# A state-space scan and a convolution stage on one core: state copies in the scan's step, x projections with rising due times, and earlier due times for turns and exponentials

## The chip, the cores and the metric

The kernel runs on one core of a Trainium2 chip. Its engines are PE (TensorE: matrix products and transpositions), DVE (VectorE), ACT (ScalarE), POOL (GpSimd) and SP (SyncE, which here only issues DMAs). They run side by side, each through its own list of instructions in order, and wait for each other by semaphores. The metric is the time of one execution in microseconds (us); the median of three runs of the kernel before is 3147.45 us (3142.55 to 3149.4).

## The reference

Two layers, both added to their input. The first normalises each image over groups of channels, treats its 32 x 32 pixels as a sequence of L = 1024 steps and runs a selective state-space model over it. The second is an attention between two 3 x 3 convolutions. Cut to what matters here (B = 4 images, C = 512 channels, 1024 inner channels, 16 states):

```python
xs = silu(causal_conv4(xm) + conv_b)               # xm, z = halves of LN(x) @ W_in
proj = xs @ W_x                                    # 32 + 16 + 16 columns
dt = softplus(proj[..., :32] @ W_dt + b_dt)
Bm, Cm = proj[..., 32:48], proj[..., 48:]
def step(h, inp):                                  # over the 1024 steps
    dA = exp(dt_t[..., None] * A)
    h = dA * h + (dt_t * x_t)[..., None] * B_t[:, None, :]
    y = einsum('bds,bs->bd', h, C_t)
    return h, y
out = ((ys + xs * D) * silu(z)) @ W_out
```

The second layer computes two 1 x 1 and one 3 x 3 convolution, a softmax over all pairs of pixels, a weighted sum, and a last 3 x 3 convolution.

## The kernel before

**The first stage** works through the images one after the other. Channels lie on the 128 partitions; the 1024 inner channels are eight blocks, taken in four pairs `e`; the sequence is cut into two halves `h` of T = 512 steps. A *chunk* is one pair and one half (8 chunks an image, 32 in all, first half and second half in turn), and in it each of the 16 states `s` is a *unit*: 512 units. A unit (function `unit`) does this:

- ACT computes the decays exp(dt A), one [128, 512] instruction for each of the two blocks (line 746).
- The input term dt x B comes in one of two ways. For the ten states of `B_ON_ACT`, ACT scales rows of a transposed copy by B (line 758) and PE transposes the result back into a PSUM tile "u" (the *turn*, line 784). For the other six, POOL multiplies by B that a DMA has spread over the partitions (line 773), and the decays go into "u".
- DVE runs the recurrence with one scan instruction for each block (line 798). In the second half it starts from the state that the first half left in `carry_sb`.
- The product with C is made by POOL for both blocks at once (line 826), or by DVE for the three states of `C_ON_DVE` (line 814). PE adds the result into the PSUM tile "y" by transposing products (line 833).

In the first half the last column of each scan has to be kept in `carry_sb`. For the three states of `C_ON_DVE` each scan is followed, in the same step, by a copy of its own column (line 803, 128 x 1). For the other thirteen a step of its own copies the columns of both blocks in one instruction (line 820, 128 x 2), when both scans are done; the product with C overwrites the tile and so comes after it.

After the 16 units of a chunk `gate` turns y back and multiplies it by the gate. Other work of the same stage fills in: for the next image the norms (`norms`), the input projection with the four taps of the causal convolution on DVE (`conv1`, line 610), the gates' projection (`gates`), and the projection of xs to dt, B and C (`params`, line 652), which sums over the eight blocks for each half into one PSUM tile "pp"; for the image before, the output projection (`out_proj`); and 32 pieces of the transform of the second stage's convolution weights on POOL (`transform`, lines 1084 to 1119). `first_image` prepares the second stage's first image: it loads it, takes its statistics and normalises it.

**What sets the order.** No instruction of this stage is issued where it is written. Each is wrapped into a step with an engine, an estimated duration, the buffers that it reads and writes, and a due time in units (`prio`; a smaller number is more urgent). `Plan.issue` then walks through a model of the five engines: it takes, on the engine that is free first, the most urgent step that can start, books its duration, and writes the instruction down. Buffers that several steps share are rings; the rings "u" (four PSUM tiles, two units' worth), "h", "dbx", "sc", "cbc" and "bb" are handed out in the order of the program. "mm" (two PSUM tiles) serves the projections, the deltas and the gates. The due times of the fill work come from the dictionary `PRM`. The order on each engine is therefore fixed when the program is built; on the chip each engine follows it and waits where the estimate was off.

**The second stage** is written in order, from line 1180 on, and isn't touched by the diff, but for an engine order at its start that follows from when the first stage's tiles come free.

Of the kernel before, what the change touches and what calls it, by code (L numbers as in the profile page):

```python
# [20 lines left out]
NDC = DI // P  # L21
NS = 16
RK = 32
T = 512
# [3 lines left out]
GS = 16  # L28


PRM = dict(fi=4.61, m0=27.7, n0=50.77, nl=1.39, q0=50.1, qg=7.76, c0=53.17, cg=7.07, p0=120.48, e0=6.38, eg=3.72, g0=78.98, gg=9.04, o0=14.48, og=4.13, dl=9.01, t0=10, tg=21.42)


class Buf:
# [135 lines left out]
def mamba_then_pab_kernel(  # L170
# [25 lines left out]
    nc = tc.nc  # L196
# [67 lines left out]
    with ExitStack() as l0:  # L264
# [48 lines left out]
        carry_sb = wp.tile([P, 2, NS], F32, tag="carry", name="carry_sb")  # L313
# [24 lines left out]
        step = plan.step  # L338
        MM, TR = 0.88, 0.114
        ROWS, EXP, SCAN = 0.8, 0.61, 1.18  # L340
# [17 lines left out]

        proj = [buf(None, proj_sb[k * NP : (k + 1) * NP], "") for k in range(2)]
        bts = [buf(None, bt_sb[k], "") for k in range(2)]  # L360
        carry = [buf(None, None, "") for s in range(NS)]
        bcds = [buf(None, t, "") for t in bcd]
        szds = [[buf(None, None, "") for d in range(NDC)] for b in range(B)]
        gds = [[[buf(None, None, "") for h in range(NH)] for k in range(2)] for b in range(B)]
# [278 lines left out]
        def params(b, prio):  # L643

            p0 = b % 2 * NP
            pr = proj[b % 2]
            for h, hs in enumerate(halves):
                pp = buf("mm" if b else f"y{h}", [P, T], f"pp_{b}_{h}")
                for d in range(NDC):
                    step(  # L650
                        "PE", MM,
                        lambda d=d, hs=hs, pp=pp: nc.tensor.matmul(
                            pp()[p0 : p0 + NP, :], wx_sb[:, d, :], xs[b, d]()[:, hs],
                            start=(d == 0), stop=(d == NDC - 1),
                        ),
                        [xs[b, k] for k in range(NDC)] if b and d == 0 else [xs[b, d]], [pp],
                        prio if b else prio - 10 + d + 0.5,
                    )
                step(
                    "ACT", 0.48,  # L660
                    lambda hs=hs, pp=pp: nc.scalar.copy(pr()[:, hs], pp()[p0 : p0 + NP, :]),
                    [pp], [pr], prio,
                )
            step(
                "SP", 0.3, lambda: nc.sync.dma_start(bcd[b], pr()[RK:NP, :]),
                [pr], [bcds[b]], prio, kb=128,
            )
            pt = buf("mm", [P, NT, NP], f"pbt_{b}")

            def turn():  # L670
                for k in range(NT):
                    nc.tensor.transpose(
                        pt()[:, k, :], pr()[:, k * P : (k + 1) * P],
                        ident[p0 : p0 + NP, p0 : p0 + NP],
                    )

            step("PE", 8 * TR, turn, [pr], [pt], prio)
            bt = bts[b % 2]
            step(
                "DVE", 0.21, lambda: nc.vector.tensor_copy(bt(), pt()[:, :, RK : RK + NS]),  # L680
                [pt], [bt], prio,
            )
# [45 lines left out]
        def unit(b, e, h, s, y):  # L728


            dt, dtx, dtxt = dts[b, e, h]
            hs = halves[h]
            name = f"{b}_{e}_{h}_{s}"
            prio = (b * NDC + 2 * e + h) * NS + s
            bc = bcds[b]
            c_bc = buf("cbc", [P, 1, T], f"cbc_{name}")
            step(
                "SP", 0.32,
                lambda: nc.sync.dma_start(c_bc()[:, 0], bcd[b][NS + s][hs].partition_broadcast(P)),
                [bc], [c_bc], prio, kb=256,  # L740
            )
            us = [buf("u", [P, T], f"u_{name}_{j}") for j in range(2)]

            def decay(j, t):
                at = (2 * e + j) * NS + s
                nc.scalar.activation(t, dt()[:, j], AF.Exp, scale=a_sb[:, at : at + 1])  # L746

            on_act, on_dve = s in B_ON_ACT, s in C_ON_DVE
            if on_act:
                bt = bts[b % 2]  # L750
                sc = buf("sc", [P, NK, 2, P], f"sc_{name}")
                hc = buf("h", [P, 2, T], f"da_{name}")
                for r in range(2):

                    def rows(r=r):
                        for k in range(2 * r, 2 * r + 2):
                            at = h * NK + k
                            nc.scalar.activation(  # L758
                                sc()[:, k], dtxt()[:, k], AF.Copy, scale=bt()[:, at, s : s + 1]
                            )  # L760

                    step("ACT", ROWS, rows, [dtxt, bt], [sc], prio)
            else:
                b_bc = buf("bb", [P, 1, T], f"bbc_{name}")
                step(
                    "SP", 0.32,
                    lambda: nc.sync.dma_start(b_bc()[:, 0], bcd[b][s][hs].partition_broadcast(P)),
                    [bc], [b_bc], prio, kb=256,
                )
                hc = buf("dbx", [P, 2, T], f"dbx_{name}")  # L770
                step(
                    "POOL", 2.31,
                    lambda: nc.gpsimd.tensor_mul(hc(), dtx(), b_bc().to_broadcast([P, 2, T])),  # L773
                    [dtx, b_bc], [hc], prio,
                )

            parts = [buf(None, None, "") for j in range(2)]
            for j, u in enumerate(us):
                part = parts[j]
                if on_act:  # L780

                    def turn(j=j, u=u):
                        for k in range(NK):
                            nc.tensor.transpose(  # L784
                                u()[:, k * P : (k + 1) * P], sc()[:, k, j, :], ident
                            )

                    step(
                        "ACT", EXP, lambda j=j: decay(j, hc()[:, j]), [dt], [part], prio, "exp",
                        holds=[hc],  # L790
                    )
                    step("PE", 4 * TR, turn, [sc], [u], prio - 1)
                else:
                    step("ACT", EXP, lambda j=j, u=u: decay(j, u()), [dt], [u], prio - 1, "exp")

                def scan(j=j, u=u):
                    ht = u() if on_dve else hc()[:, j]
                    nc.vector.tensor_tensor_scan(  # L798
                        ht, *((hc()[:, j], u()) if on_act else (u(), hc()[:, j])),
                        carry_sb[:, j, s : s + 1] if h else 0.0, ALU.mult, ALU.add,  # L800
                    )
                    if h == 0 and on_dve:
                        nc.vector.tensor_copy(carry_sb[:, j, s : s + 1], ht[:, T - 1 : T])

                before, behind = ([carry[s]], []) if h else ([], [carry[s]] if on_dve else [])
                step(
                    "DVE", SCAN + (0.15 if behind else 0.0), scan,
                    [part if on_act else hc, u, *before],
                    [u if on_dve else part, *behind], prio - 1, holds=[hc],
                )  # L810
                if on_dve:
                    step(
                        "DVE", 0.6,
                        lambda j=j, u=u: nc.vector.tensor_mul(hc()[:, j], u(), c_bc()[:, 0]),
                        [u, c_bc], [part], prio, holds=[hc],
                    )
            if h == 0 and not on_dve:
                step(
                    "DVE", 0.15,
                    lambda: nc.vector.tensor_copy(carry_sb[:, :, s], hc()[:, :, T - 1]),  # L820
                    parts, [carry[s]], prio - 1, holds=[hc],
                )
            if not on_dve:
                step(
                    "POOL", 2.31,
                    lambda: nc.gpsimd.tensor_mul(hc(), hc(), c_bc().to_broadcast([P, 2, T])),  # L826
                    [c_bc], parts, prio, holds=[hc],
                )
            for j in range(2):

                def add(j=j):
                    for k in range(NK):
                        nc.tensor.matmul(  # L833
                            y[j]()[:, k, :], hc()[:, j, k * P : (k + 1) * P], ident,
                            start=(s == 0 and k == 0), stop=(s == NS - 1 and k == NK - 1),
                            is_transpose=True, skip_group_check=True,
                        )

                step("PE", 4 * TR, add, [parts[j]], [y[j]], prio, holds=[hc])

        def gate(b, e, h, y):

# [304 lines left out]
        for b in range(B):  # L1147
            at = b * NDC * NS
            for n in range(NDC):
                e, h = divmod(n, NH)  # L1150
# [401 lines left out]
```

## Time and profile before

| | |
|---|---|
| median of three runs | 3147.45 us |
| the profiled execution: time, span | 3152.2 us, 3150.4 us |
| first stage, from the first scan to the last | 166 to 2092 us |
| busy over the span: PE, DVE, ACT, POOL | 2801.1, 2324.9, 1896.9, 2185.6 us |
| granted TensorE clock, mean | 0.968 of full speed |
| DVE scans (L798), 128 x 512 | 1024, about 1.20 us in the first half, 1.26 in the second |
| POOL products of 128 x 1024 (L826, L773) | 608, 2.37 us each |
| DVE copies to `carry_sb`, 128 x 2 (L820) | 208, 83.8 us from "da" and 43.3 us from "dbx" |
| DVE copies to `carry_sb`, 128 x 1 (L803) | 96, 0.158 us each |

The span runs from the first to the last instruction, and the time lies around it. A line number such as L820 is the line of the kernel that issued an instruction. In an answer about waits, "A <- B: 47.4, 33, 7.5" means that A stood idle for B 47.4 us in total, 33 times, at most 7.5 us. In the tables of instructions the numbers after the tile names are the shortest, median and longest duration in ns, or the start and the duration in us in a timeline. [...]

### The profile page before, as it was taken

What the parts mean: (1) busy time and instruction counts of PE and PEld (TensorE: products, weight loads), DVE (VectorE), ACT (ScalarE), POOL (GpSimd) and SP (SyncE); (2) the same over time, 40 slices, a digit from 0 to 9 for tenths busy, and PEclk for the clock granted to TensorE, in tenths of its full rate; (3) what the DMA queues carried; (4) which work ended last, traced back from release to release, by engine and by line L of the source; (5) the groups of instructions that cost most, each with busy time, mean ns of one, the idle gap of its engine ahead of it and who ended that gap; (6) DMA issues with size and microseconds to landing.
All of it is one profiled execution on the core that took longest, in us unless ns stands there. A gap on an engine that the chain in (4) does not pass through costs nothing. (4 is left out here: it accounts for less than half of the span.)

```text
span 3150.4 us, 36613 instructions
## 1 busy us (share of the span) xinstructions
PE 2801.1 (89%) x11832; PEld 1654.8 (53%) x11832; DVE 2324.9 (74%) x2746; ACT 1896.9 (60%) x3322; POOL 2185.6 (69%) x1207
## 2 busy tenths in 40 slices
PE   4988878989888999888999877779999999999998
PEld 2455656666556656565655655544444444444443
DVE  3488899988999988999987987876275366447344
ACT  3499889998799999789998787752030030020000
POOL 8899898999969999978899998853052142224222
PEclk8999899999999999999999989989999999999999
DMA  6666455577645567745567654457268448628817
GB/s 190 192 186 195 144 152 162 156 226 241 212 118 169 163 204 250 231 114 155 165 192 227 204 172 123 121 139 263 93 225 312 183 147 317 257 74 312 321 61 253
DMA packets 401414, 600.03 MB, mean 190 GB/s; under 512 B 47176, under 2 KB 241992, under 8 KB 376648
## 3 DMA queue, kind: packets, MB, share of 16 engines
q1 hardware_dynamic: 392128, 582.13, 58.8%
q10 hardware_dynamic: 8936, 15.31, 1.3%
q8 instruction: 94, 1.54, 0.2%
q14 instruction: 96, 0.79, 0.1%
q0 software_dynamic: 160, 0.26, 0.0%
HBM read 500.60 MB, written 96.99 MB: 190 GB/s over the span
## 5 line engine op out<-in xcount | busy, mean ns | idle before, releaser
L826 POOL TENSOR_TENSOR da<-da,cbc 128x1024 f32<-128x1024 f32 x288 | 679.4, 2364 | 87.2 <-DVE carry_sb L820 47.4
L758 ACT ACTIVATE sc<-dtxt,bt_sb 128x256 f32<-128x256 f32 x1280 | 557.1, 496 | 49.3 <-PE u L784 48.8
L746 ACT ACTIVATE da<-dt,a_sb 128x512 f32<-128x512 f32 x640 | 439.4, 713 | 70.1 <-PE y L833 69.5
L773 POOL TENSOR_TENSOR dbx<-dtx,bbc 128x1024 f32<-128x1024 f32 x192 | 452.1, 2367 | 30.6 <-DMA bbc<-bcd 8.3
L784 PE MATMUL u<-ident,sc 128*128 128x128 f32 x2560 | 380.6, 282 | 52.4 <-DVE da L798 31.7
L833 PE MATMUL y<-ident,da 128*128 128x128 f32 x2560 | 357.3, 283 | 70.7 <-POOL da L826 68.2
L798 DVE TENSOR_TENSOR_SCAN da<-da,carry_sb,u 128x512 f32<-128x512 f32 x288 | 353.3, 1260 | 82.8 <-PE u L784 82.6
L833 PEld LDWEIGHTS y<-ident,da 128*128 128x128 f32 x2560 | 297.6, 145 | 183.4 <-POOL da L826 134.2
L784 PEld LDWEIGHTS u<-ident,sc 128*128 128x128 f32 x2560 | 302.2, 144 | 160.3 <-issue 41.7
L798 DVE TENSOR_TENSOR_SCAN da<-da,u 128x512 f32<-128x512 f32 x288 | 337.1, 1202 | 37.3 <-PE u L784 37.2
L1389 PE MATMUL m_b<-uw_b,v_b 128*128 128x512 f32 x768 | 339.1, 599 | 10.3 <-DMA uw_b<-u_b 9.4
L1389 PE MATMUL m_o<-uw_o,v_o 128*128 128x512 f32 x768 | 333.5, 595 | 4.3 <-DVE v_o L1311 4.1
L826 POOL TENSOR_TENSOR dbx<-dbx,cbc 128x1024 f32<-128x1024 f32 x128 | 302.8, 2365 | 32.1 <-DVE carry_sb L820 22.6
L381 PE MATMUL pxm<-xt,winc 128*128 128x344 f32 (+2 forms) x768 | 249.6, 469 | 30.5 <-DVE xs L610 13.9
L746 ACT ACTIVATE u<-dt,a_sb 128x512 f32<-128x512 f32 x384 | 252.9, 679 | 34.8 <-DVE da L798 18.9
L833 PE MATMUL y<-ident,dbx 128*128 128x128 f32 x1536 | 217.1, 281 | 43.7 <-POOL dbx L826 31.6
L381 PE MATMUL pz<-xt,winc 128*128 128x512 f32 x512 | 246.2, 599 | 10.5 <-ACT sz L631 3.1
L1389 PEld LDWEIGHTS m_b<-uw_b,v_b 128*128 128x128 f32 x768 | 144.7, 191 | 197.8 <-issue 185.7
L1389 PEld LDWEIGHTS m_o<-uw_o,v_o 128*128 128x128 f32 x768 | 145.5, 190 | 190.5 <-issue 181.2
L833 PEld LDWEIGHTS y<-ident,dbx 128*128 128x128 f32 x1536 | 178.4, 144 | 98.2 <-POOL dbx L826 48.6
L1437 PE MATMUL pat<-y_b,st 128*128 128x512 f32 x512 | 221.7, 593 | 0.1
L1397 ACT ACTIVATE e_b<-m_b 128x512 f32<-128x512 f32 x24 | 14.3, 596 | 320.6 <-PE m_b L1389 299.4
(231 smaller groups left out, 4536.2 us busy)
## 6 DMA issues: line engine op xcount, KB each, us to landing
cbc<-bcd SPq DMA_DIRECT2D x512, 256.0 KB, 3.7
uw_b<-u_b SPq DMA_DIRECT2D x96, 1024.0 KB, 4.9
uw_o<-u_o SPq DMA_DIRECT2D x96, 1024.0 KB, 4.9
bbc<-bcd SPq DMA_DIRECT2D x192, 256.0 KB, 4.1
u_b<-work SPq DMA_DIRECT2D x192, 128.0 KB, 2.3
u_o<-work SPq DMA_DIRECT2D x192, 128.0 KB, 3.1
winc<-in_w_in_dram SPq DMA_DIRECT2D x64, 256.0 KB, 3.8
szd<-sz SPq DMA_DIRECT2D x32, 512.0 KB, 3.6
```

The lines of the kernel that those rows point to most:

```text
L381: lambda k=k, lhs=lhs, rhs=rhs: nc.tensor.matmul(p()[:, at : at + cols], lhs(), rhs(), start=(k == 0), stop=(k == n - 1)),
L746: nc.scalar.activation(t, dt()[:, j], AF.Exp, scale=a_sb[:, at : at + 1])
L758: nc.scalar.activation(sc()[:, k], dtxt()[:, k], AF.Copy, scale=bt()[:, at, s : s + 1])
L773: lambda: nc.gpsimd.tensor_mul(hc(), dtx(), b_bc().to_broadcast([P, 2, T])),
L784: nc.tensor.transpose(u()[:, k * P : (k + 1) * P], sc()[:, k, j, :], ident)
L798: nc.vector.tensor_tensor_scan(ht, *((hc()[:, j], u()) if on_act else (u(), hc()[:, j])), carry_sb[:, j, s : s + 1] if h else 0.0, ALU.mul ...
L826: lambda: nc.gpsimd.tensor_mul(hc(), hc(), c_bc().to_broadcast([P, 2, T])),
L833: nc.tensor.matmul(y[j]()[:, k, :], hc()[:, j, k * P : (k + 1) * P], ident, start=(s == 0 and k == 0), stop=(s == NS - 1 and k == NK - 1), ...
L1389: nc.tensor.matmul(m[q], v[:, q, k, c, :], w[:, c, :], start=(c == 0), stop=(c == NCC - 1 and not extra),)
L1397: nc.scalar.activation(e, m[2], AF.Copy, scale=al / 2)
L1437: nc.tensor.matmul(pt, st[m][:, 2 * P * j + h : 2 * P * (j + 1) : 2], xb[m // 2][:, m % 2, :], start=(m == 0), stop=(m == NMC - 1),)
```

## The change

- **State copies.** The separate step of line 820 is gone. In the first half each scan's step now ends with a copy of its own last column (128 x 1) for every state; `carry` becomes one buffer for each state and block. The step's estimated duration is the scan's plus 0.14 for all states.
- **x projections.** In `params`, for images 1 to 3, the 16 matmuls of an image no longer share one due time: each is due 0.6 units after the one before (`pg`), from 112 units (`p0`, 120.48 before), and the copies to `proj` and what follows are due at the end of that.
- **Turns and exponentials.** The turns are due 2 units ahead of their unit (`kt`), the exponentials that go into "u" 1.91 units (`ke`); both were due 1 ahead. The additions to y are due 0.1 units later (`ka`).
- **Due times.** Eleven weight transforms instead of ten are due in the prologue (`t0`), `first_image` is due 21.48 units before the end instead of 4.61 (`fi`), and other entries of `PRM` move by small amounts (`fl` is used nowhere).

```diff
-PRM = dict(fi=4.61, m0=27.7, n0=50.77, nl=1.39, q0=50.1, qg=7.76, c0=53.17, cg=7.07, p0=120.48, e0=6.38, eg=3.72, g0=78.98, gg=9.04, o0=14.48, og=4.13, dl=9.01, t0=10, tg=21.42)
+PRM = dict(pg=0.6, kt=2, ke=1.91, ka=-0.1, fl=12.26, fi=21.48, m0=27.24, n0=50.77, nl=2.01, q0=44.34, qg=7.76, c0=53.52, cg=6.79, p0=112, e0=6.38, eg=2.48, g0=78.98, gg=9.04, o0=14.48, og=4.24, dl=9.01, t0=11, tg=21.45)
...
-        carry = [buf(None, None, "") for s in range(NS)]
+        carry = [[buf(None, None, "") for j in range(2)] for s in range(NS)]
...
-                        prio if b else prio - 10 + d + 0.5,
-                    )
+                        prio + PRM["pg"] * (d + NDC * h) if b else prio - 10 + d + 0.5,
+                    )
+                end = prio + (PRM["pg"] * NDC * (h + 1) if b else 0)
...
-                    [pp], [pr], prio,
-                )
+                    [pp], [pr], end,
+                )
+            prio = end
...
-                    step("PE", 4 * TR, turn, [sc], [u], prio - 1)
+                    step("PE", 4 * TR, turn, [sc], [u], prio - PRM["kt"])
                 else:
-                    step("ACT", EXP, lambda j=j, u=u: decay(j, u()), [dt], [u], prio - 1, "exp")
+                    step("ACT", EXP, lambda j=j, u=u: decay(j, u()), [dt], [u], prio - PRM["ke"], "exp")
...
-                    if h == 0 and on_dve:
+                    if h == 0:
                         nc.vector.tensor_copy(carry_sb[:, j, s : s + 1], ht[:, T - 1 : T])
 
-                before, behind = ([carry[s]], []) if h else ([], [carry[s]] if on_dve else [])
-                step(
-                    "DVE", SCAN + (0.15 if behind else 0.0), scan,
+                before, behind = ([carry[s][j]], []) if h else ([], [carry[s][j]])
+                step(
+                    "DVE", SCAN if h else SCAN + 0.14, scan,
...
-            if h == 0 and not on_dve:
-                step(
-                    "DVE", 0.15,
-                    lambda: nc.vector.tensor_copy(carry_sb[:, :, s], hc()[:, :, T - 1]),
-                    parts, [carry[s]], prio - 1, holds=[hc],
-                )
...
-                step("PE", 4 * TR, add, [parts[j]], [y[j]], prio, holds=[hc])
+                step("PE", 4 * TR, add, [parts[j]], [y[j]], prio - PRM["ka"], holds=[hc])
```

## The prediction

> **What bounds the kernel now.** I read the page first: in its forty slices the first 26 or so (the state-space stage, 0 to about 2092 us) have four engines between 80 and 100% busy at once, and the rest (convolution and attention) is PE alone. The change touches only the first part, so I cut that by batch with the table by stage (columns: us, then busy us of PE, PE weight loads, DVE, ACT, POOL, then clock and DMA).
>
> ```profile
> core 0: us, PE busy (x) PEld busy (x) DVE busy (x) ACT busy (x) POOL busy (x), PEclk, DMA share, GB/s
> 166.00:655.00 489.00, 423.57 (x2287) 291.86 (x2286) 436.24 (x518) 448.66 (x778) 444.09 (x243) 0.95 0.58 169
> 655.00:1147.00 492.00, 439.39 (x2358) 297.49 (x2357) 445.74 (x531) 440.06 (x769) 447.32 (x242) 0.98 0.61 185
> 1147.00:1637.00 490.00, 436.78 (x2359) 296.40 (x2357) 444.92 (x530) 439.00 (x768) 445.70 (x241) 0.98 0.62 186
> 1637.00:2092.00 455.00, 369.27 (x2079) 256.63 (x2078) 392.80 (x441) 349.01 (x648) 407.26 (x207) 0.95 0.60 172
> 2092.00:2123.00 31.00, 22.97 (x60) 11.43 (x58) 13.83 (x29) 10.59 (x18) 8.11 (x5) 0.74 0.25 82
> ```
>
> No engine owns a batch: ACT 92%, POOL 91%, DVE 91%, PE 89%. A batch takes 40 to 50 us more than its fullest engine, because steps come late for each other. So a saving on one engine counts only in part, and what matters is who is late. The waits between 166 and 2092 us (in total, times, longest):
>
> ```profile
> DVE da L798 <- PE u L784: 119.8, 42, 20.8
> ACT da L746 <- PE y L833: 69.5, 51, 4.9
> POOL da L826 <- DVE carry_sb L820: 47.4, 33, 7.5
> POOL dbx L826 <- DVE carry_sb L820: 22.6, 17, 5.3
> ACT u L746 <- DVE da L798: 18.9, 24, 1.6
> ```
>
> DVE waits for turns, and POOL for state copies. Looked at one by one, fourteen POOL waits of 1.5 to 7.5 us make 55 of the 70 us. Most lie where convolution taps, norms or products stand between the scans on DVE, and the copy in each takes 0.17 us or less: there DVE is late, not the copy. The view of the carry tile says what else copies cost:
>
> ```profile
> L820 DVE COPY carry_sb<-da x144: 157/242/2666, 168.6 to 2034.4; 128x2 f32<-128x2 f32 x144
> L803 DVE COPY carry_sb<-u x96: 157/158/163, 170.4 to 2021.1; 128x1 f32<-128x1 f32 x96
> L820 DVE COPY carry_sb<-dbx x64: 156/239/2366, 178.6 to 2028.2; 128x2 f32<-128x2 f32 x64
> ```
>
> A copy of two elements takes anything from 0.16 to 2.67 us, a copy of one never over 0.163. The timeline shows why: the copy of 942.01 ends when POOL's pair of multiplications ends (944.35), and the next scan waits behind it.
>
> ```profile
> 939.65 2.32 DVE L798 TENSOR_TENSOR_SCAN dbx<-u,dbx 128x512 f32<-128x512 f32 x2
> 942.01 2.37 DVE L820 COPY carry_sb<-dbx 128x2 f32<-128x2 f32 x1
> 944.29 2.32 DVE L798 TENSOR_TENSOR_SCAN da<-da,u 128x512 f32<-128x512 f32 x2
> ...
> 939.67 4.68 POOL L826 TENSOR_TENSOR da<-da,cbc 128x1024 f32<-128x1024 f32 x2
> ...
> 895.29 1.22 DVE L798 TENSOR_TENSOR_SCAN u<-u,dbx 128x512 f32<-128x512 f32 x1
> 896.54 0.16 DVE L803 COPY carry_sb<-u 128x1 f32<-128x1 f32 x1
> 896.62 1.22 DVE L798 TENSOR_TENSOR_SCAN u<-u,dbx 128x512 f32<-128x512 f32 x1
> ```
>
> **The Trainium skill.** "SBUF — State Buffer", Who interferes with whom: a DVE instruction in a two-port mode and a GpSimd instruction lock each other out for a whole instruction, copies among them. "VectorE: DVE Perf Modes", What auto-detection actually checks: a single-source copy within SBUF takes the two-port mode when its outermost dimension longer than one is even. A two-element copy qualifies; that a one-element copy doesn't is my reading, and the rows above agree with both (2666 against 163 ns). The same page, The DRAIN you can't avoid: DVE drains after every instruction, and reading what the previous one wrote takes a wait. The trace agrees: two scans without carry follow each other at 1.13 us, a scan and its own copy take 1.33.
>
> **The change part by part**, against the profiled execution (span 3150.4, time 3152.2 us).
>
> *State copies.* In first-half chunks, 13 of 16 states lose the joint copy of two elements (16 chunks x 13 = 208 instructions) and get one single-element copy after each scan (416); DVE issues 208 more. Busy time: 127.0 us of joint copies (83.8 + 43.3) against 416 x 0.158 = 65.7. Occupancy counts, since a copy also holds up the next scan: where a pair of scans and its joint copy run without a gap, start to next start is 2.81 us in the mean (median 2.51, longest 4.92), against 2 x 1.33 = 2.66. Saved: 208 x 0.15 = 31 us of DVE. The usual unit becomes 0.15 us longer; the blocked ones win up to 2.2. DVE and POOL are equally full, so I put half on the path: -16. Ends: 0 (POOL or ACT sets the pace) and -31.
>
> *Turns and exponentials ahead.* Turns (due one unit ahead) become due two ahead, exponentials of the GpSimd-scaled states 1.91 ahead; nothing is added. The DVE waits for turns are 119.8 us, less the opening one of 20.8: 99. They can't all go: the four "u" buffers hold just two units, and between 1100 and 1147 us PE itself is busy 46.56 of 47 us. I take a third, 33 us of DVE, half on the path: -16. Ends 0 and -50. Behind a turn that waits for a buffer stand the y additions, for which ACT's next exponentials wait (69.5 us); behind an early exponential the scaled rows that feed the next turns. That is the slower rival.
>
> *x projections.* The same 32 PE passes a batch (about 16 us at 0.5) run, by the changed program's order, over units 105-121 instead of 111-121 in batch 0, and 235.5-249 instead of 243-249 in batch 1; the copy to "proj", the store to "bcd", its transposition and the next deltas still follow at their end. Two or three us of PE leave the crowded last chunk: -5 for three batches. Against it, a projection tile holds one of the two "mm" buffers some 7 units longer; with about five handovers more at one copy (0.575) and a gap (0.2) each it is 4 us a batch, +12 at worst. Ends +12, -15.
>
> *Prologue.* One more weight transform stands before the first dtx on POOL (11 against 10): 12.3 us into a gap of 10.4 us (141.5 to 151.9). POOL has 10 us less to do later, its first dtx is 2 late: -5. Ends 0, -10. Its DMAs leave SP in the same prologue; their number in all stays.
>
> *First image.* Its 8 loads on SP, 4 memsets on POOL, 12 statistics, 4 normalisations come before the last chunk's scans on DVE instead of after them. Off the join: the table loads and root that held PE for 4.6 us at 2107, and statistics ahead of the last gate; -7. But 5.6 + 3.0 us of DVE work enter a last chunk in which DVE is already 100% busy, with 9 us of idle DVE in the chunk before to absorb part: +5. In the next stage's order the input transform of the first convolution comes behind two more POOL operations of about 2.5 us and interleaves with the maxima: +2. Sum 0; ends -9, +8.
>
> *Norms, convolutions and gates* move by a few units (batch 1's norms 6 units earlier with wider steps; its gates end 8 units earlier). The same instructions; they fill gaps between scans, so 0. If that cover went, a norm's 16 DVE operations of 0.74 us, 12 us, would be exposed once.
>
> Sum: -16 - 16 - 5 - 5 + 0 = -42: a span of 3108 and a time of 3110. The profiled execution lies 4.75 over the median of the runs (3147.45), so the median is **3106 us**, 1.3% less.
>
> **Rivals.** (1) *Larger gain*: late DVE work is what leaves POOL idle (70 us), and the blocked copies made it late. If POOL ran 95% of each batch, as it already does in good stretches (48.13 of 50 us from 1150), the four batches take 1744 / 0.95 = 1836 instead of 1926: -90, 3058. Against: ACT would have to run at 96% in batch 0. (2) *No gain that shows*: the DVE time freed turns into DVE idling, because ACT (448.66 of 489) and POOL need their time anyway; 3147. Against: the copies lie in front of POOL's largest waits. (3) *Slower*: exponentials of the GpSimd-scaled states get in line early and wait at ACT's head for a "u" buffer, which DVE must free. Today 26.7 us of such waits in 38 (18.9 + 7.8 for the other kind), 0.7 us each, of 384 exponentials. Of 96 in a batch, if 60% wait, it is 40 us a batch, what ACT has spare; beyond that each adds to the time. At 80%, 54 us, some 14 us too much in three batches of ACT-heavy work: 3147 + 42 less half the other gains, 3168. Against: the planner's order lets ACT take other ready steps first. (4) That the copies don't lose their blocking is excluded by the 96 rows of one-element copies.
>
> **How the numbers follow.** Mine 0.60 (its own range 3080 to 3138: ends of the parts, not all at once), larger gain 0.22, no gain 0.07, slower 0.11. So faster by over 0.2% (below 3141) is 0.82, within it 0.07, slower 0.11; 0.2% is about what a measurement of this kernel can tell from no change. The range 3055 to 3142 takes the larger gain and leaves out no gain and slower.
>
> **What would show it.** Right: all copies of carry at 128x1 and 0.157 to 0.163 us, about 80 us of DVE in all with the 96 old ones; DVE's wait for turns under 80 us; POOL's wait behind carry copies about halved; batches of about 480 us; after the last scan, scores starting within 25 us instead of 31.6. Wrong: ACT waits for "u" above 60 us, PE waits for "mm", batches still near 490 with DVE idling more.

## The result, and the profile after

The changed kernel takes 3105.64 us in the median of four runs (3100.51 to 3108.2); the kernel before, run beside it, 3148.43 (3142.55 to 3156.02). The ratio is 0.9861, with a 95% interval of 0.9836 to 0.9886. That is 0.4 us from the forecast. The experiments show that the sum came out right, but not its parts.

The table by stage of the changed kernel, cut at its own batches (columns as before: us, then busy us of PE, PE weight loads, DVE, ACT, POOL, then clock and DMA):

```profile
core 0: us, PE busy (x) PEld busy (x) DVE busy (x) ACT busy (x) POOL busy (x), PEclk, DMA share, GB/s
163.00:649.00 486.00, 429.39 (x2300) 296.02 (x2299) 423.71 (x571) 454.92 (x787) 442.48 (x242) 0.95 0.59 170
649.00:1129.00 480.00, 436.71 (x2354) 301.88 (x2353) 430.48 (x582) 436.22 (x765) 449.79 (x244) 0.97 0.64 191
1129.00:1604.00 475.00, 438.97 (x2359) 304.68 (x2358) 430.55 (x582) 436.63 (x766) 444.52 (x241) 0.96 0.64 192
1604.00:2058.00 454.00, 369.87 (x2071) 254.13 (x2070) 394.30 (x513) 350.46 (x649) 395.01 (x199) 0.95 0.58 167
```

The span is 44.1 us shorter (3150.4 to 3106.3). By the starts of the scans, 3.0 of it lie before the first scan (166.2 to 163.2), 30.8 in the four batches (489.2, 491.9, 490.0, 454.2 became 485.8, 480.2, 474.9, 453.6, so nearly all in the second and third), and the rest after the last scan (1058.9 to 1048.7). DVE works 12 to 15 us less in each of the first three batches; there ACT and POOL have about the work that they had.

The waits of the changed kernel between 163 and 2058 us (in total, times, longest), those that answer to the rows shown of before:

```profile
DVE da L800 <- PE u L786: 102.6, 45, 20.6
ACT da L748 <- PE y L829: 55.1, 44, 5.1
POOL da L822 <- DVE carry_sb L805: 35.7, 24, 5.3
POOL dbx L822 <- DVE carry_sb L805: 22.9, 12, 6.0
ACT u L748 <- DVE da L800: 8.9, 13, 1.6
```

Four of the five are smaller, one (22.6 before) is as large as it was, none is gone: DVE's wait for turns fell from 119.8 to 102.6 us, POOL's for state copies, both rows together, from 70.0 to 58.6. The view of the carry tile:

```profile
L805 DVE COPY carry_sb<-da x288: 152/154/158, 164.4 to 1994.9; 128x1 f32<-128x1 f32 x144
L805 DVE COPY carry_sb<-dbx x128: 152/154/156, 173.6 to 1988.4; 128x1 f32<-128x1 f32 x128
L805 DVE COPY carry_sb<-u x96: 157/158/160, 167.1 to 1980.7; 128x1 f32<-128x1 f32 x96
```

There are 512 copies instead of 304, and none takes over 0.160 us, although 412 of them start and end inside one POOL instruction. This also settles what the rows of before left open. There all 96 one-element copies read the PSUM tile "u", so they differed from the two-element copies in the memory that they read as well as in the number of elements. Here 416 copies read "da" and "dbx" in SBUF, 328 of them inside a POOL instruction, and they take 0.152 to 0.158 us. The timeline shows two of them: both copies lie inside POOL's pair of products, 885.02 to 889.69, and neither is held up.

```profile
885.01 1.21 DVE L800 TENSOR_TENSOR_SCAN da<-da,u 128x512 f32<-128x512 f32 x1
886.26 0.15 DVE L805 COPY carry_sb<-da 128x1 f32<-128x1 f32 x1
886.33 1.21 DVE L800 TENSOR_TENSOR_SCAN da<-da,u 128x512 f32<-128x512 f32 x1
887.57 0.15 DVE L805 COPY carry_sb<-da 128x1 f32<-128x1 f32 x1
...
885.02 4.67 POOL L775 TENSOR_TENSOR dbx<-dtx,bbc 128x1024 f32<-128x1024 f32 x2
```

### The profile page after: what moved, and what is told of

Read it like the earlier page. It is cut to its first block, busy times and chain, and to the rows that moved or that the text cites. A ratio compares the mean times of both kernels' runs of the same rounds, so it can differ in the third digit from the quotient of the medians.

```text
span 3106.3 us, 36781 instructions
## 1 busy us (share of the span) xinstructions
PE 2799.1 (90%) x11832; PEld 1666.2 (54%) x11832; DVE 2259.1 (73%) x2954; ACT 1893.6 (61%) x3321; POOL 2175.4 (70%) x1207
## 4 chain that ended last, share of the span: by engine, by line
PE 42%; DVE 16%; POOL 6%; issue 4%; ACT 4%; DMA 4%; SPq 0%; POOLq 0%; DVEq 0%; ACTq 0%
PE m_o L1385 9%; PE m_b L1385 8%; PE pat L1433 7%; DVE da L800 6%; PE y L829 4%; PE po L381 3%; DVE dbx L800 3%; PE pz L381 2%; PE u L786 2%; DMA uw_b<-u_b 2%; DVE u L800 2%; POOL da L822 2%; PE psc L1265 2%; ACT sc L760 1%; POOL dbx L822 1%
## 5 line engine op out<-in xcount | busy, mean ns | idle before, releaser
L800 DVE TENSOR_TENSOR_SCAN da<-da,u 128x512 f32<-128x512 f32 x288 | 349.2, 1212 | 48.1 <-PE u L786 44.8
L381 PE MATMUL pxm<-xt,winc 128*128 128x341 f32 (+2 forms) x768 | 244.2, 462 | 18.0 <-ACT xt L557 9.0
L829 PE MATMUL y<-ident,dbx 128*128 128x128 f32 x1536 | 223.6, 286 | 25.8 <-POOL dbx L822 17.9
```

Source lines behind the costliest of these rows:

```text
L381: lambda k=k, lhs=lhs, rhs=rhs: nc.tensor.matmul(p()[:, at : at + cols], lhs(), rhs(), start=(k == 0), stop=(k == n - 1)),
L800: nc.vector.tensor_tensor_scan(ht, *((hc()[:, j], u()) if on_act else (u(), hc()[:, j])), carry_sb[:, j, s : s + 1] if h else 0.0, ALU.mul ...
L829: nc.tensor.matmul(y[j]()[:, k, :], hc()[:, j, k * P : (k + 1) * P], ident, start=(s == 0 and k == 0), stop=(s == NS - 1 and k == NK - 1), ...
```

## The experiments

The diff does two things that come together in the profile: it alters the copies, and, through its due times and the planned length of the steps, it alters the order on every engine. So the first group of runs holds the order fixed and alters the copy alone; the second alters due times; the third alters the order and nothing else. No experiment leaves any of the computation out. All ratios are to the kernel before, measured beside the run.

### The copy alone, with the order of every engine held

**1. The order before, the joint copy replaced by two copies of one column at the same place.**

```diff
-                    lambda: nc.vector.tensor_copy(carry_sb[:, :, s], hc()[:, :, T - 1]),
+                    lambda: [
+                        nc.vector.tensor_copy(carry_sb[:, j, s : s + 1], hc()[:, j, T - 1 : T])
+                        for j in range(2)
+                    ],
```

> The kernel before, in its own order on every engine; only the joint two-element copy is replaced by two one-element copies at the same place. Theory A (a two-element copy waits for POOL's instruction, and the scans behind it pay): no copy over 0.17 us, DVE gains about 0.25 us a unit (2.81 against two scans at 1.13 and two short copies, about 2.56), 52 us in all, half of it on the path: 15 to 30 us faster than before. Theory B (the order that the planner makes is what pays, the copies were covered): within 6 us of before.

Measured: 3105.21 us (3100.97 to 3108.67), ratio 0.987 (0.9857 to 0.9884), against 3145.34. The copy alone, with no due time touched, brings 40 us: as much as the whole change, and more than the 15 to 30 expected. DVE is busy 2247.3 us instead of 2324.9. The carry tile of this kernel:

```profile
L821 DVE COPY carry_sb<-da x288: 120/144/156, 164.6 to 1986.2; 128x1 f32<-128x1 f32 x144
L821 DVE COPY carry_sb<-dbx x128: 125/143/156, 173.8 to 1980.2; 128x1 f32<-128x1 f32 x128
```

And DVE's waits for turns in it, which are as large as before:

```profile
DVE da L798 <- PE u L784: 126.2, 45, 21.1
```

**2. The changed order, with a joint copy in the step of the second block's scan.**

```diff
-                    if h == 0:
+                    if h == 0 and on_dve:
                         nc.vector.tensor_copy(carry_sb[:, j, s : s + 1], ht[:, T - 1 : T])
+                    if h == 0 and not on_dve and j == 1:
+                        nc.vector.tensor_copy(carry_sb[:, :, s], hc()[:, :, T - 1])
```

> The changed kernel in its own order on every engine, but the thirteen states that had a joint two-element copy have it again, in the step of the second block's scan. A: copies of 0.16 to 2.6 us come back, and the kernel is 10 to 25 us slower than the changed one (about 3120 to 3130). B: within 6 us of the changed kernel (about 3105).

Measured: 3156.72 us (3151.01 to 3162.89), ratio 1.0034 (1.0022 to 1.0047). With all else of the change in place the joint copy makes it slower than before: 51 us behind the changed kernel, where 10 to 25 were expected. DVE is busy 2345.3 us. The carry tile, and the timeline round the longest copy:

```profile
L807 DVE COPY carry_sb<-da x144: 168/224/3341, 169.9 to 2049.8; 128x2 f32<-128x2 f32 x144
L807 DVE COPY carry_sb<-dbx x64: 168/245/2380, 179.7 to 2043.7; 128x2 f32<-128x2 f32 x64
```

```profile
781.92 2.31 DVE L800 TENSOR_TENSOR_SCAN da<-da,u 128x512 f32<-128x512 f32 x2
784.26 3.34 DVE L807 COPY carry_sb<-da 128x2 f32<-128x2 f32 x1
787.52 1.22 DVE L800 TENSOR_TENSOR_SCAN u<-u,dbx 128x512 f32<-128x512 f32 x1
...
782.86 4.72 POOL L824 TENSOR_TENSOR da<-da,cbc 128x1024 f32<-128x1024 f32 x2
```

The copy starts in the first of two products that follow each other on POOL, and ends with the second (787.60 and 787.58); the next scan stands behind it for over 3 us.

**3 and 4. One copy of both columns that isn't a copy instruction**: a maximum over a dimension of length 1, which moves the same two elements, first in the changed order, then in the order before.

```diff
-                        nc.vector.tensor_copy(carry_sb[:, :, s], hc()[:, :, T - 1])
+                        nc.vector.reduce_max(carry_sb[:, :, s], hc()[:, :, T - 1 : T], axis=AX.X)
```

> As the run before, but the two last columns are taken by one maximum over a dimension of length one, a reduction instead of a copy. If only the copy's two-port mode is blocked by POOL (A), this instruction stays at about 0.16 us and comes once in a unit: pair and copy at about 2.46 us instead of 2.66, 42 us less of DVE, half on the path, 10 to 25 us faster than the changed kernel (about 3085 to 3095). B: the same as the changed kernel. If reductions are blocked too: as with the joint copy.

> The kernel before in its own order, with the joint copy made by a reduction over a dimension of length one (one instruction, not held up by POOL). Theory A' (about half of each us of DVE saved is gained): DVE as in the run with two single copies (a pair with its copies 2.44 us in both), so about 3105. Against the changed kernel with the same reduction (3092) it shows what the new due times alone are worth once the copies are no matter: 13 us if A' holds.

Measured: in the changed order 3092.34 us (3089.53 to 3096.94), ratio 0.9831 (0.9818 to 0.9845), faster than both kernels; in the order before 3104.29 (3102.16 to 3106.45), ratio 0.9871 (0.9857 to 0.9884). The carry tile of the former:

```profile
L807 DVE TENSOR_REDUCE carry_sb<-da x144: 156/157/160, 164.9 to 1979.2; 128x2 f32<-128x2 f32 x144
L807 DVE TENSOR_REDUCE carry_sb<-dbx x64: 156/157/159, 173.6 to 1971.6; 128x2 f32<-128x2 f32 x64
```

Same two elements, same place, same neighbours on POOL: 0.160 us at most instead of 3.341. So with two elements it is the kind of instruction that decides: the copy is held up, the reduction isn't. With copies it is the number of elements: two are held up, one isn't (run 1). The Trainium skill ("SBUF — State Buffer", Who interferes with whom) says that on this chip a reduction has no two-port mode and never contends with GpSimd, while a copy can; these two runs agree with both halves.

Together (us; a cell is the median of its kernel):

| form of the copy | order before | changed order |
|---|---|---|
| joint, 128 x 2 | 3147.45 | 3156.72 |
| two of 128 x 1 (changed order: each behind its own scan) | 3105.21 | 3105.64 |
| joint, as a reduction | 3104.29 | 3092.34 |

Down a column the order is the same. Across the first and the third row the copy is the same; in the middle row its place differs too, so that row doesn't show the order alone. Down, the copy is worth 40 us in the order before (3145.34 beside it) and 51 in the changed one. Across, the other parts of the change together cost some 11 us with the joint copy and bring 12 with the reduction.

Two reservations. The changed kernel was measured in another session than runs 1 to 3, and the kernel before read 3.1 us higher in it; by the ratios the 51 us are 54, and the 13 us from the changed kernel to run 3 are 9. And the granted clock goes along with the times: 0.960 to 0.961 in run 2, 0.967 to 0.970 in the changed kernel, 0.972 to 0.973 in run 3. For the same work in the four batches PE was busy 12 us longer in run 2 than in the changed kernel, and 19 us less in run 3. Whether that is a part of the cause or a consequence isn't shown.

### Parts of the due times

**5. The copies alone, as the change makes them, with all due times of before**: the changed code with `kt=1, ke=1, ka=0, pg=0` and the other entries of `PRM` as they were.

> The own copy in each scan's step with its planned 0.14 us, and all due times as before: the planner makes a new order. The prediction: -16 us against before, ends 0 and -31. B: the gain of the copies alone is nothing, within 6 us of before.

Measured: 3144.44 us (3134.67 to 3149.0), ratio 0.9995 (0.9988 to 1.0002): no gain. The copies are as short as in the changed kernel (none over 0.16 us). Against run 1 two things differ: the place of the first block's copy, and the order, which the planner worked out anew. So when the planner works the order out anew, the copies alone bring nothing, and the due times on top of them bring 39 us (3144.44 to 3105.64); with the order held it is the other way round. What a part of the change is worth depends on the order in which it stands. The joint copy wasn't run in this order, so what the form of the copy is worth there isn't known.

**6. The changed kernel without the look-ahead.**

```diff
-PRM = dict(pg=0.6, kt=2, ke=1.91, ...
+PRM = dict(pg=0.6, kt=1, ke=1, ...
```

> The changed kernel with turns and exponentials due one unit ahead again (kt and ke at 1), all else as changed. The prediction: the look-ahead is worth 16 us (0 to 50), so about 3121, and the waits of DVE for turns go up from 82 us by about a third. Rival (the order as such is luck): anywhere within 15 us on either side, with no more waits for turns.

Measured: 3138.9 us (3132.9 to 3151.26), ratio 0.9981 (0.997 to 0.9992). Taking the look-ahead away costs 33 us. POOL now waits 98.8 us behind state copies instead of 58.6, and DVE for turns 106.9 instead of 102.6: the waits by which this part was priced hardly move.

```profile
DVE da L800 <- PE u L786: 106.9, 53, 20.5
POOL da L822 <- DVE carry_sb L805: 84.2, 33, 10.6
POOL dbx L822 <- DVE carry_sb L805: 14.6, 9, 3.5
```

**7. The look-ahead alone, on the kernel before**: `kt=2, ke=1.91`, all else as before, joint copies in their own step.

> The kernel before with one part of the change alone: turns and exponentials two units ahead; joint copy, projections, first image and all other due times as before. Theory 1 (the form of the copy and the look-ahead each pay by themselves): the look-ahead is worth about what its removal from the changed kernel cost, 33 us, so 3105 to 3125 us, with the DVE's waits for turned tiles well below the 120 us of before. Theory 2 (the look-ahead pays only once the copies no longer hold the DVE up, because until then the scans are late for another reason): 3138 to 3152 us, with the joint copies still at a mean of 200 ns and more.

Measured: 3177.89 us (3176.71 to 3184.65), ratio 1.0104 (1.0088 to 1.0121), against 3147.62. By itself it makes the kernel 30 us slower, which neither theory had. DVE is as busy as before (2327.6 and 2324.9 us), and so are its state copies (143.7 and 142.2), so these aren't held up more; all four batches are longer (494.4, 500.1, 499.6, 462.6). The granted clock was lower, 0.961 to 0.963 against 0.968 to 0.972, and PE was busy 18 us longer in the four batches; what is cause here and what consequence isn't shown.

**8. The x projections as before**: the changed kernel with `pg=0, p0=120.48`.

> The changed kernel with all sixteen x projections of an image due at once at 120.48 units again. The prediction: spreading is worth 5 us (from 15 gained to 12 lost), so about 3110. Rival: the two PSUM tiles held longer cost more than the spreading gives, and this is faster than the changed kernel by up to 12 us.

Measured: 3120.52 us (3115.14 to 3125.58), ratio 0.9924 (0.9911 to 0.9938): 15 us slower than the changed kernel.

**9. The first image as before**: the changed kernel with `fi=4.61`.

> The changed kernel with the first image due 4.61 units before the end again; the order differs only in the last quarter of the stage. The prediction: nothing in sum (7 us gained at the join, 5 lost in the last chunks, 2 in the first convolution), so within 6 us of 3105. By the trace of the changed kernel the time from the last scan to the end is 10 us shorter than before (1048.6 against 1058.9 us) and the last two chunks are 6 us longer (115.5 against 109.0): this run should give both back, 0 to 5 us slower.

Measured: 3105.04 us (3101.12 to 3106.94), ratio 0.9872 (0.9858 to 0.9885): no difference. In the profile both halves of the trade can be seen. The last two chunks take 109.7 us instead of 115.4, and what follows the last scan 1055.5 instead of 1048.7.

**10. All the changed due times, with the joint copy in its own step**, planned anew.

> All the changed due times, look-ahead, spreading and first image, but the joint 128x2 copy in its own step as before, and the order planned anew. Theory 1 (the copies' form is most of the gain, and the due times are worth some 12 us, as the two orders differ with the one-instruction copy that is not held up): 3130 to 3140 us. Theory 2 (the due times only serve the order with own copies, as the joint copy put into the changed order gave 3157): 3145 to 3160 us. Theory 3 (the due times are most of the gain): 3105 to 3120 us.

Measured: 3162.25 us (3156.66 to 3165.28), ratio 1.0047 (1.0032 to 1.0062). All due times without the copies make it 15 us slower, as run 2 did by 11 in another order.

### The order and nothing else

**11. The same work, planned with another number**: the own copy is planned at 0.15 us instead of 0.14.

```diff
-                    "DVE", SCAN if h else SCAN + 0.14, scan,
+                    "DVE", SCAN if h else SCAN + 0.15, scan,
```

> The changed kernel with one number of the planner altered: the own copy is planned at 0.15 instead of 0.14 us. No work differs, only the order on each engine. Theory 1 (an order that comes out differently by chance moves the time by less than 0.2%): 3099 to 3112 us. Theory 2 (the due times fit one order, and any other order loses part of the gain): 3115 to 3140 us; then differences of 10 to 30 us between kernels with different orders can't be put down to a part of the change.

Measured: 3127.82 us (3123.75 to 3129.71), ratio 0.9938 (0.9924 to 0.9952): 22 us slower than the changed kernel, with the same work (only ACT loads a function table 174 times instead of 176) and the same granted clock (0.966 to 0.970). 428 of 2442 positions on DVE, copies apart, hold another instruction. The table by stage shows the work spread over longer batches.

```profile
653.00:1139.00 486.00, 438.43 (x2362) 299.25 (x2359) 430.63 (x583) 433.61 (x765) 437.34 (x232) 0.97 0.62 186
1139.00:1623.00 484.00, 434.77 (x2352) 298.53 (x2352) 430.79 (x582) 434.69 (x763) 443.70 (x240) 0.97 0.63 188
```

In the second batch DVE has 430.63 us of work, 430.48 in the changed kernel, ACT 433.61 against 436.22, and POOL 12 us less, of which 7 were done in the first batch; yet it takes 485.4 us instead of 480.2, the third 484.8 instead of 474.9. This is the price of another order, which nobody chose. The variants of the changed kernel whose orders the planner worked out anew in runs 5, 6, 8 and 10 are slower than it by 15 to 57 us, and run 7 is 30 slower than the kernel before. Each holds the effect of its part and of such another order together, and one order for each can't tell the two apart. None of these orders came out faster than the one it is compared with, so the scatter isn't even to both sides: the changed kernel has a good order among those that were tried, and why it is good isn't shown.

**12. The reduction, with the planner told of it**: the first block's scan planned without a copy, the second's with 0.14 us, the order worked out anew.

```diff
-                    "DVE", SCAN if h else SCAN + 0.14, scan,
+                    "DVE", SCAN + (0.14 if not h and (on_dve or j) else 0.0), scan,
```

> The changed kernel with one copy of both columns as a maximum over a dimension of length 1, behind the second block's scan, and the planner told so: the first block's scan planned without a copy, the second's with 0.14 us; the order is planned anew. Theory 1 (a plan that counts what the DVE really does gives an order at least as good): 3075 to 3092 us. Theory 2 (the order matters by chance as much as by plan): 3092 to 3125 us; the copies themselves 156 to 160 ns in either case.

Measured: 3117.11 us (3115.67 to 3122.97), ratio 0.9911 (0.9895 to 0.9927). A plan that is closer to what DVE does came out 25 us slower than run 3, whose order was planned for other copies. That is the second theory, and the second sight of what another order costs.

## Why the prediction was right, and where it was not

**The number was right, and that it was so close is luck: the copies brought far more than they were given, the rest less, by about as much.** The sum was -16 for the copies and -26 for all else: -16 for the look-ahead, -5 for the projections, -5 for the prologue and 0 for the rest. Measured with the order held, the copies are worth -40 to -51, outside their ends of 0 and -31. One path takes the two parts in turn: from the kernel before to run 2 everything changes but the form of the copy, +11; from run 2 to the changed kernel that form alone, -51. By the table the rest is +11 to -12, and -26 was predicted. On the other path, where the planner makes a new order at each step, the copies are worth -1 (run 5) and the due times -39. Neither path gives the shares of the sum.

**State copies: mechanism right, half on the path about right, size of the DVE term wrong.** That two-element copies are held up by POOL and one-element copies aren't is shown by runs 1 and 2, and runs 3 and 4 show that it takes the copy instruction. One step of the argument was not sound, though it came out true: the 96 one-element copies of before couldn't exclude rival (4), since they all read PSUM. "Half on the path" held up: 40.1 us for 77.6 of DVE (0.52) in run 1, 41.0 for 87.9 (0.47) in run 4, 51.1 for 86.2 (0.59) from run 2 to the changed kernel, 13.3 for 28.7 (0.46) from there to run 3. By the ratios the last two are 0.63 and 0.33; and from run 1 to run 4 DVE has 10 us less and the time is the same within 1 us. So half is a rough mean, not a rule.

What failed is "208 x 0.15 = 31 us of DVE". It set the pitch of the joint copy in the order before, 2.81 us, against two scans each with its own copy. (Pitch is the time from the start of one pair of scans to the start of the next, where they run without a gap.) Two effects are netted in it. Where both single copies stand behind the second scan, the pitch is 2.44 (run 1), so not being held up is worth 208 x 0.37 = 77 us, which is what DVE lost. Putting each copy behind its own scan gives 208 x 0.21 = 44 us back (2.65 in the changed kernel). And in the changed order joint copies would have been held up more: pitch about 3.07 in run 2, 208 x 0.42 = 87 us over 2.65, for 86 measured. So the step used a pitch that belonged to the old order for a kernel that has a new one. "The blocked ones win up to 2.2" was low too: up to 3.2 in run 2.

**Turns and exponentials: not confirmed.** The step took 33 us of DVE's waits for turns and put half on the path. The waits fell by 17 (119.8 to 102.6), and run 1, in the order before with single copies, has 126.2 us of them and the time of the changed kernel. So this wait doesn't set the time by itself. The two runs that isolate the look-ahead contradict each other: its removal cost 33 us, adding it alone cost 30. Either it pays only where the scans aren't late for another reason, or both numbers are mostly the effect of whatever order came out. This stays open; it would take several orders of each kind.

**x projections**: -5 predicted, 15 us lost when undone, at its predicted end but inside the 22 us that run 11 shows for nothing at all. Not settled.

**Prologue**: the first scan came 3.0 us sooner, but with the order of before it starts at 162.3 us in run 1 and at 165.8 in run 4. These 3 us lie within what executions differ by, so the -5 is not shown. In the fourteen kept traces they go with the granted clock before the first scan: it starts at 161.8 to 163.2 us where that clock was 0.93 or 0.94, and at 165.8 to 167.6 where it was 0.90 or 0.91, in both orders.

**First image: right in both halves.** Sum 0 predicted and 0.6 measured in run 9. +5 for the last chunk was +5.8 in the last two chunks; -7 at the join with +2 for the first convolution was -6.8 after the last scan. The order of the first three batches is the same in both kernels, so this one difference isn't clouded by the planner.

**The signs that were named.** Right: copies all at 128x1, 79.1 us of DVE in all (about 80); batches of 486, 480, 475 (about 480); scores 20.3 us after the last scan (within 25). Wrong: the wait for turns at 102.6 us (under 80), or 82.0 without its longest, which is the opening one, as the prediction counted; POOL's wait behind copies 58.6 (half of 70 would be 35). Of the signs of a wrong prediction one came for the first batch alone: 485.8 us, near 490, with DVE idle for 62 us of it instead of 53. The others did not: ACT's waits for "u" behind the scans of "da" fell from 18.9 to 8.9 us, so the slower rival, with waits piling up at ACT's head, did not happen; and PE's waits ahead of the products of the projections and gates fell from 69 to 51. The larger gain rested on POOL's 70 us going away; they did not, and even run 3, with the copies as short as they get, keeps 52 us of them and takes 3092.

## What to carry to other kernels

A tiny instruction has no tiny price if it can be locked out by another engine: look at the longest duration in its row beside the median, and for a few elements use a form that isn't held up, such as a reduction over a length of 1 or copies of single elements behind the last of their producers. When a change alters both an instruction and the order that a planner writes down, hold the order and alter the instruction; only then is the difference its own. And before a part of a schedule is given credit for 20 us, plan the same work with a number altered by a hair: here that alone moved the time by 22.

## What the runs showed of the hardware that was not expected

- In the kernel before, 159 of the 208 joint copies took over 0.175 us, and each of them ended 0.022 to 0.030 us after the end of a POOL instruction. So most of them were held up, over half of these (87) for less than 0.2 us; the median in the rows of before (0.24 us) is already a held-up copy.
- A copy that is held up doesn't always get in between two products that follow each other on POOL. In run 2 two copies that started in the middle of a product ended with the one behind it, after 3.19 and 3.34 us, against 2.36 for one product; in the kernel before the longest copy (2.67 us) did so, begun 0.33 us before the end of its product.
- Two single copies side by side behind the second scan take 0.14 us each, and scan, scan, copy, copy has a pitch of 2.44 us: as much as with one reduction (2.44), and 0.21 less than scan, copy, scan, copy (2.65). A scan with another scan behind it has a pitch of 1.13, one with its own copy behind it 1.33. This fits a wait of some 0.2 us for a result just written, paid once for a pair or twice; it wasn't measured by itself. Of a pause after every instruction the records show nothing: a scan with another scan behind it lasts 1.20 us, and the next one's record begins 0.07 us before its end.
- The first batch differs by 6.8 us between executions of the same order of instructions in it: 485.8 us at a mean clock of 0.95 in the changed kernel, 479.0 at 0.97 in run 9. Differences of a few us in that batch are not read here.
